# Clears cut into row slices, the lead's tap weights in the scans' PSUM banks, and one FFN group of the last image as a 1x1 convolution with VectorE taps

## The chip, the cores and the metric

The kernel runs on one core of one Trainium2 chip. The metric is device time in microseconds (us). Three runs of the kernel before gave 30005.71, 30010.10 and 30014.66 us, so the median is 30010.1 us. The profile comes from one more execution, which took 29956.3 us.

## The reference, cut to what matters

Eight images of 64 channels and 128x128 pixels pass through two layers. All arithmetic is float32.

```python
# layer 0: every pixel gets nine softmax weights; "high" is the negated weighted sum of its 3x3 window plus the pixel
h = leaky(conv3x3(x, w1, b1))
w_hp = delta_center - softmax(conv1x1(h, w2, b2), axis=1)
x = x + sum(shifted(x, k) * w_hp[:, k:k+1] for k in range(9))
# layer 1
x_norm = layernorm_over_channels(x)
seq = layernorm(tokens(x_norm))                      # 16384 tokens of 64 channels
for i in range(2):                                   # two blocks, each a scan forwards and one backwards
    seq = bimamba_block(seq, ...)                    # 128 inner channels x 16 states
x4 = conv3x3(image(rmsnorm(seq)), resconv_w) + res
dw = depthwise3x3(conv1x1(x_norm, dw1_w), dw2_w)
x = x + dw * x4
xn = layernorm_over_channels(x)
g = depthwise3x3(conv1x1(xn, ffn_in_w), ffn_dw_w)    # 64 -> 340 channels, each with its own nine taps
g1, g2 = split(g)                                    # 170 channels each
return x + conv1x1(gelu(g1) * g2, ffn_out_w)         # 170 -> 64
```

## The kernel before, in words

**Steps.** All work after the weights' preparation is entered into a table with `at(time, phase, fn)` and then issued in sorted order of time and phase. The phases are FEED, SCAN, MID, PROD, DECAY and REST, in that order. Each engine executes its own instructions in exactly this order, and so does the queue of SyncE (SP), which issues every DMA. A step has no fixed length: where an instruction waits, everything behind it on its engine waits too.

**Scans.** One image is 64 chunks of 16 steps (1024 steps). A chunk is 1024 tokens in one direction of one block. GpSimd (POOL) forms eight products per chunk (`drive`, L991), ScalarE (ACT) sixteen exponentials (`decay`, L999) into PSUM tiles of the pool `ps_w` (tag `w`, two tiles of 128x1024, each two banks), VectorE (DVE) sixteen scans (L1017 and L1019), and DVE or POOL multiplies with C (L1041, L1038). `dtx` (L947) overwrites a chunk's `dt` on POOL after that tile's copy to DRAM has landed.

**Front, Mix and FFN** are the convolutional stages. Each is 16 chunks of eight rows: two halves of 4x128 pixels, one on the lower 64 partitions and one on the upper 64. Front (layer 0 and the first norms) of image b+1, and Mix and FFN of image b, run beside scans. The exceptions are Front of image 0, which starts at step -199 while the first scan products start at step -5, and FFN of the last image, which starts at step 1084 of that image while its scans end at step 1024. Such a stage is called alone here.

**PSUM.** Beside the two `w` tiles there are four single banks: `y` (scan outputs), `mm` (projections), `bg` and `acc` (convolutional stages). A pool hands out a bank again once the last reader of the tile before is done.

**Front's taps.** For each of nine taps `weight` (L498 to L500) spreads one row of softmax weights over the channels with a matmul into the bank `bg`; `weighted` (L504) multiplies the shifted window with it on DVE; `gather` (L510) adds the product into `acc` with an identity matmul. `bg` also holds the tile `ms` of the norms.

**FFN.** The weights of 1x1 and depthwise convolution are multiplied into one 3x3 convolution from 64 to 340 channels. These come in groups: group 0 is the first 128 channels of g1, group 1 the first 128 of g2, and group 2 the remaining 42 of each. A window tile holds a window on its lower 64 partitions and the same window shifted by one pixel on the upper 64, so that one matmul makes two taps (`wpair`, L746) and the third is made from 64 partitions (`wlast`, L752). A float32 matmul stands as two records in the profile. Alone, a group's two PSUM halves lie in one `w` tile; order and times for a chunk that starts at step a are: group 0 at a, group 2 at a+3, GELU at a+5, group 1 at a+6, products with GELU's result at a+9, `project` (L777 to L786) at a+12. Chunks follow each other every 12 steps. The weights of a stage are one tile, `bgw`, loaded from DRAM by `load_weights` (L428).

**Clears.** Zero-padded images lie in DRAM as 64 channels of 131 rows of 130 pixels. `clear` (L88) writes zeros over a whole one with one DMA from a 130-wide tile: `x` first of all, `dw0` at step -199, `xm` at 64, `xn` at 128, `dw1` at 192.

## Time and profile before

| what | value |
|---|---|
| median of three runs | 30010.1 us |
| the profiled execution | 29956.3 us |
| its span in the profile | 29954.4 us |
| PE, DVE, ACT, POOL busy | 81%, 90%, 62%, 92% of the span |
| first scan product (L991) | 567.8 us after the span's start |
| FFN alone: first matmul to the span's end | 29447.9 to 29954.4 us |

Busy time is the time in which an engine had an instruction in work. A wait line names the engine and instruction that waited, what released it, the microseconds in total, how often, and the longest. A row of a stretch gives each engine's busy microseconds with its number of instructions, then the clock that TensorE was granted as a share of full speed, the mean busy share of the 16 DMA engines, and GB/s. Rows marked SPq are DMA issues. In a group's line "128*64 128x512" means a contraction over 128 partitions, 64 output partitions, and a moving operand of 512 columns.

### The profile page before, as it was taken

The numbers are of one execution on the slowest core, as the hardware profiler recorded it, in microseconds if no ns is written. First come the engines' busy times: TensorE is split into PE (matmuls) and PEld (weight loads), VectorE is DVE, ScalarE is ACT, GpSimd is POOL, SyncE is SP. The second block draws the span as 40 slices with busy tenths as digits, with TensorE's granted clock in tenths as the row PEclk, the third lists the DMA queues.
The fourth block names the chain that finished last, engine by engine and source line by source line (L and its number), as shares of the span: only waits on it lengthen the run. The fifth ranks groups of instructions, "written<-read, shape, count | busy, mean of one in ns | idle before, by whom it ended". The sixth has DMA issues, their size and how long they took to land. (4 is left out here: it accounts for less than half of the span.)

```text
span 29954.4 us, 307972 instructions
## 1 busy us (share of the span) xinstructions
PE 24257.7 (81%) x96344; PEld 8093.1 (27%) x96344; DVE 27086.6 (90%) x17258; ACT 18533.8 (62%) x28316; POOL 27661.8 (92%) x8732
## 2 busy tenths in 40 slices
PE   7666888878888788887888788887888878888579
PEld 3211232223322233222322223222232223322123
DVE  3899999999999999999999999999999999999992
ACT  2566666666666666666666666666666666666661
POOL 3999999999999999999999999999999999999991
PEclk8777888988989888988899889898898988889789
DMA  4776676766777677776777767776677766777672
GB/s 100 210 241 214 221 235 230 237 213 223 237 231 237 213 225 237 232 232 210 233 232 238 225 214 232 232 237 223 215 236 232 240 214 222 235 234 234 214 240 75
DMA packets 2529698, 6617.29 MB, mean 221 GB/s; under 512 B 417862, under 2 KB 722262, under 8 KB 2525750
## 3 DMA queue, kind: packets, MB, share of 16 engines
q1 hardware_dynamic: 2528054, 6597.59, 68.4%
q8 instruction: 761, 12.47, 0.2%
q14 instruction: 883, 7.23, 0.1%
HBM read 5363.40 MB, written 1266.10 MB: 221 GB/s over the span
## 5 line engine op out<-in xcount | busy, mean ns | idle before, releaser
L991 POOL TENSOR_TENSOR bu<-dup,bp 128x2048 f32<-128x2048 f32 x4096 | 18578.8, 4539 | 557.7 <-DVE w L1019 421.4
L999 ACT ACTIVATE w<-dtp,a_neg 128x1024 f32<-128x1024 f32 x8192 | 9162.3, 1118 | 510.2 <-DVE hs L1017 313.9
L1038 POOL TENSOR_TENSOR hs<-hs,cp 128x1024 f32<-128x1024 f32 x2832 | 6685.3, 2361 | 197.9 <-ACT state L1031 133.3
L1041 DVE TENSOR_TENSOR hs<-w,cp 128x1024 f32<-128x1024 f32 x5360 | 6564.9, 1225 | 310.9 <-DMA cp<-bc_dram 77.6
L1017 DVE TENSOR_TENSOR_SCAN w<-w,state,bu 128x1024 f32<-128x1024 f32 x2677 | 6280.9, 2346 | 346.5 <-ACT w L999 345.9
L1019 DVE TENSOR_TENSOR_SCAN w<-w,state,bu 128x1024 f32<-128x1024 f32 x2683 | 6291.0, 2345 | 314.1 <-ACT w L999 313.5
L1057 PE MATMUL y<-hs,sel_y 128*32 128x512 f32 x32768 | 5183.3, 702 | 33.0 <-POOL hs L1038 32.6
L1031 ACT COPY state<-w 128x1 f32<-128x1 f32 x5360 | 837.4, 156 | 5040.0 <-DVE hs L1041 5004.5
L1017 DVE TENSOR_TENSOR_SCAN hs<-w,state,bu 128x1024 f32<-128x1024 f32 x1419 | 3321.3, 2341 | 86.4 <-ACT w L999 36.9
L1019 DVE TENSOR_TENSOR_SCAN hs<-w,state,bu 128x1024 f32<-128x1024 f32 x1413 | 3307.7, 2341 | 52.8 <-ACT w L999 34.7
L1050 PE MATMUL y<-xc,dskip 128*64 128x512 f32 x4096 | 1622.3, 860 | 2025.6 <-ACT yv L1074 1339.3
L869 PE MATMUL xp<-hn,wx 128*128 128x512 f32 x4096 | 2269.2, 682 | 485.3 <-ACT xc L875 339.8
L746 PE MATMUL fp<-fw,bgw 128*128 128x512 f32 (+1 forms) x6144 | 2353.9, 638 | 64.7 <-ACT ga L759 63.5
L1057 PEld LDWEIGHTS y<-hs,sel_y 128*32 128x32 f32 x32768 | 736.8, 116 | 3496.6 <-issue 2469.7
L1031 ACT COPY state<-hs 128x1 f32<-128x1 f32 x2832 | 540.2, 191 | 1829.2 <-DVE hs L1019 929.6
L414 POOL TENSOR_TENSOR r<-r,neg_half 128x8 f32<-128x8 f32 x768 | 1263.5, 1645 | 380.5 <-ACT r L411 323.9
L875 ACT ACTIVATE xc<-xp,cbias 128x512 f32<-128x512 f32 x1024 | 697.2, 681 | 1415.1 <-PE xp L869 1414.7
L910 PE MATMUL dp<-xc,wdt 128*128 128x512 f32 x2048 | 1228.5, 684 | 351.8 <-ACT dt L917 268.2
L752 PE MATMUL fp<-fw,bgw 64*128 64x512 f32 (+1 forms) x6144 | 1501.1, 608 | 0.0
L999 ACT ACT_TABLE_LOAD x1134 | 1454.9, 1283 | 20.1
L947 POOL TENSOR_TENSOR dt<-dt,xc 128x1024 f32<-128x1024 f32 x512 | 1212.8, 2369 | 246.5 <-DMA dt_dram<-dt 223.8
L510 PE MATMUL acc<-t,ident 128*128 128x512 f32 x2304 | 1361.3, 675 | 0.0
(184 smaller groups left out, 26903.7 us busy)
## 6 DMA issues: line engine op xcount, KB each, us to landing
bp<-bc_dram SPq DMA_DIRECT2D x4096, 256.0 KB, 4.0
dup<-du_dram SPq DMA_DIRECT2D x4096, 256.0 KB, 5.0
dtp<-dt_dram SPq DMA_DIRECT2D x4096, 256.0 KB, 5.0
cp<-bc_dram SPq DMA_DIRECT2D x4096, 256.0 KB, 5.0
hn<-hn_dram SPq DMA_DIRECT2D x1024, 256.5 KB, 4.8
dt_dram<-dt SPq DMA_DIRECT2D x512, 512.0 KB, 3.1
du_dram<-dt SPq DMA_DIRECT2D x512, 512.0 KB, 2.6
yf_dram<-yv SPq DMA_DIRECT2D x512, 256.0 KB, 4.4
```

Of the source, the lines that this page charges most:

```text
L746: nc.tensor.matmul(o, wpair[:, i, g, m], self.win[h][:, i : i + ROWS, 0:W], start=(i == 0), stop=False)
L752: nc.tensor.matmul(o, wlast[rows, i, g, m], self.win[h][rows, i : i + ROWS, lo : W + lo], start=False, stop=(i == 2),)
L869: nc.tensor.matmul(self.xp[h], wx[:, self.l, self.d, i, :], self.hn2[:, s.start + 2 * i : s.stop + 2 * i], start=(i == 0), stop=(i == 1),)
L991: nc.gpsimd.tensor_tensor(bu, self.dup[self.pairs[k][1]], self.over_pair("bp", k), ALU.mult)
L999: nc.scalar.activation(w, self.dtp[gp][:, i, :], AF.Exp, scale=a_neg[:, self.l, self.d, g, j : j + 1])
L1017: nc.vector.tensor_tensor_scan(to, w, bu, s0, ALU.mult, ALU.add)
L1019: nc.vector.tensor_tensor_scan(to[:, ::-1], w[:, ::-1], bu[:, ::-1], s0, ALU.mult, ALU.add)
L1031: nc.scalar.copy(self.column(u), h[:, T - 1 : T] if self.d == 0 else h[:, 0:1])
L1038: nc.gpsimd.tensor_tensor(hs, hs, c, ALU.mult)
L1041: nc.vector.tensor_tensor(hs, w, c, ALU.mult)
L1050: nc.tensor.matmul(self.y[C * h : C * h + C, :], dskip[:, self.l, self.d, C * gp : C * gp + C], self.xc[:, s], start=True, stop=False,)
L1057: nc.tensor.matmul(self.y[lo : lo + 32, :], sel_y, hs[:, i, s], start=False, stop=(k % 4 == 3))
```

## The change

- **Clears.** `clear` takes a range of rows. Each of the four images is written in 15 DMAs of nine rows (the last has five): `dw0` from step -219 every 2 steps, `xm` from 64, `xn` from 192 and `dw1` from 320, every 8 steps.
- **Front.** The chunks 0 to 7 of image 0, whose taps end ahead of step -2, put two taps' weights into one tile of tag `w`, by halves, in place of `bg`.
- **FFN of the last image.** Group 2 is no longer a 3x3 convolution on TensorE. `before_taps` makes its 1x1 convolution over the six rows of both windows into four banks (`acc`, `bg`, `mm`, `y`), ACT copies them to SBUF, and DVE makes nine taps for each of the two sets of 42 channels. The residual is added by DVE in place of an identity matmul. Chunks follow every 8 steps, the weights are loaded at step 1074 in place of 1080, and their tile and its preparation hold the 1x1 weights and taps in addition.

```diff
-LAST_MIX_STEP, LAST_MIX_AT, LAST_FFN_STEP, LAST_FFN_AT = 16, 826, 12, 1084
+LAST_MIX_STEP, LAST_MIX_AT, LAST_FFN_STEP, LAST_FFN_AT = 16, 826, 8, 1084
...
-    def clear(img):
+    def clear(img, lo=0, hi=PW + 1):
         nc.sync.dma_start(
-            img.rearrange("c (r w) -> c r w", w=PW),
-            zero.rearrange("c (o w) -> c o w", o=1).to_broadcast([C, PW + 1, PW]),
+            img.rearrange("c (r w) -> c r w", w=PW)[:, lo:hi],
+            zero.rearrange("c (o w) -> c o w", o=1).to_broadcast([C, hi - lo, PW]),
         )
...
-    FRONT_W, MIX_W, FFN_W = 9 * 64 + P, 18 * P, 18 * P + 2 * C
+    FRONT_W, MIX_W, FFN_W = 9 * 64 + P, 18 * P, 18 * P + 2 * C + P + 2 * 9
...
+            if g == 2:
+                nc.scalar.copy(win_b[:, c0 : c0 + n], turned(fn[0:n, :], ident[0:n, 0:n], C, n)[0:C, 0:n])
+                for h in range(2):
+                    k0 = 9 * (c0 > 0)
+                    nc.sync.dma_start(wtap_b[C * h : C * h + n, k0 : k0 + 9], fd[r0 : r0 + n, :])
...
         def weight(self, k):
-            self.wb = bg_tile("wb")
+            if not self.alone:
+                self.wb = bg_tile("wb")
+            else:
+                if k % 2 == 0:
+                    self.wbs = pw.tile([P, T], F32, tag="w", name="wb")
+                self.wb = self.wbs[:, N * (k % 2) : N * (k % 2) + N]
+            self.wbk[k] = self.wb
...
+            self.alone = a + FRONT_STEP < -2
...
+        def before_taps(self):
+            _, _, _, _, win_b, _ = ffn_weights(Bg.weights)
+            self.banks = [acc_tile("f1"), bg_tile("f1"), mm_tile("f1"), py.tile([P, N], F32, tag="y", name="f1")]
+            for i, bank in enumerate(self.banks):
+                lo = C * (i < 2)
+                for h in range(2):
+                    r0 = 3 * (i % 2)
+                    nc.tensor.matmul(
+                        bank[C * h : C * h + C, 0 : 3 * PW], win_b[:, lo : lo + C],
+                        self.win[h][0:C, r0 : r0 + 3, :], start=True, stop=True,
+                    )
+
+        def before_taps_out(self):
+            self.pre = wk.tile([P, 2, T], F32, tag="hs", name="f1", bufs=3)
+            for i, bank in enumerate(self.banks):
+                lo = 3 * PW * (i % 2)
+                nc.scalar.copy(self.pre[:, i // 2, lo : lo + 3 * PW], bank[:, 0 : 3 * PW])
+
+        def taps(self, i):
+            _, _, _, _, _, wtap_b = ffn_weights(Bg.weights)
+            win = self.pre[:, i, 0 : (ROWS + 2) * PW].rearrange("p (r w) -> p r w", w=PW)
+            o = tmp("gt" if i == 0 else "ct")
+            for k in range(9):
+                w = wtap_b[:, 9 * (1 - i) + k : 9 * (1 - i) + k + 1]
+                if k == 0:
+                    nc.vector.tensor_scalar(as_rows(o), tap(win, k), w, None, ALU.mult)
+                else:
+                    nc.vector.scalar_tensor_tensor(as_rows(o), tap(win, k), w, as_rows(o), ALU.mult, ALU.add)
...
-                nc.tensor.matmul(o[h], wout_b[rows, :], self.gt[rows, :], start=False, stop=False)
-            nc.tensor.matmul(self.op, ident, self.o, start=False, stop=True)
+                nc.tensor.matmul(o[h], wout_b[rows, :], self.gt[rows, :], start=False, stop=self.alone)
+            if not self.alone:
+                nc.tensor.matmul(self.op, ident, self.o, start=False, stop=True)
 
         def add(self):
-            nc.scalar.copy(self.o, self.op)
+            if self.alone:
+                nc.vector.tensor_tensor(self.o, self.o, self.op, ALU.add)
+            else:
+                nc.scalar.copy(self.o, self.op)
...
             if self.alone:
-                groups = ((0, 0, self.first_out, 2), (3, 2, None, 0), (6, 1, self.times, 9))
-                gelus, out = 5, 12
+                at(a - 6, REST, self.before_taps)
+                at(a - 5, DECAY, self.before_taps_out)
+                at(a - 5, REST, self.taps, 0)
+                at(a - 2, REST, self.taps, 1)
+                groups = ((0, 0, self.first_out, 2), (3, 1, self.times, 6))
+                gelus, out = 3, 9
...
-        at(a - 4, REST, load_weights, 2)
+        at(a - (10 if step == LAST_FFN_STEP else 4), REST, load_weights, 2)
...
-    for t, img in ((FIRST_FRONT_AT, dw_img[0]), (64, xm_img), (128, xn_img), (192, dw_img[1])):
-        at(t, REST, clear, img)
+    rows = -(-(PW + 1) // NCH)
+    for t, step, img in ((FIRST_FRONT_AT - 20, 2, dw_img[0]), (64, 8, xm_img), (192, 8, xn_img), (320, 8, dw_img[1])):
+        for i in range(NCH):
+            lo, hi = rows * i, min(rows * i + rows, PW + 1)
+            if lo < hi:
+                at(t + step * i, REST, clear, img, lo, hi)
```

More of the change, by code (lines that the diff above doesn't have):

```diff
@@ L177, in ffn_weights @@
         v = t[:, 0 : 18 * P].rearrange("p (i r g m) -> p i r g m", i=2, r=3, m=P)
-        return v[:, 0], v[:, 1], t[:, 18 * P : 18 * P + C], t[:, 18 * P + C : FFN_W]
+        o = 18 * P + 2 * C
+        return v[:, 0], v[:, 1], t[:, o - 2 * C : o - C], t[:, o - C : o], t[0:C, o : o + P], t[:, o + P : FFN_W]
     with tc.tile_pool(name="wspill", bufs=1) as fp, tc.tile_pool(name="wprep", bufs=2) as pp, \
@@ L184 @@
         dw2, wres = mix_weights(wt[1])
-        wpair, wlast, wout_a, wout_b = ffn_weights(wt[2])
+        wpair, wlast, wout_a, wout_b, win_b, wtap_b = ffn_weights(wt[2])
         def twice(src, n, m, k=1):
@@ L436, in __init__ @@
             self.n1, self.n2, self.n3 = Norm(), Norm(), Norm()
-            self.t = {}
+            self.t, self.wbk, self.alone = {}, {}, False
         def load_x(self, name):
@@ L503, in weighted @@
             self.t[k] = tmp("t")
-            nc.vector.tensor_tensor(as_rows(self.t[k]), tap(self.xb, k), as_rows(self.wb), ALU.mult)
+            nc.vector.tensor_tensor(as_rows(self.t[k]), tap(self.xb, k), as_rows(self.wbk.pop(k)), ALU.mult)
         def gather(self, k):
@@ L726, in conv @@
         def conv(self, g, part):
-            wpair, wlast, _, _ = ffn_weights(Bg.weights)
+            wpair, wlast, _, _, _, _ = ffn_weights(Bg.weights)
             if part == 0 and self.alone:
@@ L755, in conv @@
                     )
+        def before_taps(self):
[24 more added lines that the diff above has]
+                    nc.vector.scalar_tensor_tensor(as_rows(o), tap(win, k), w, as_rows(o), ALU.mult, ALU.add)
+            if i == 0:
+                self.gt = o
+            else:
+                self.rest = [None, o]
         def first_out(self, h):
@@ L761, in gelus @@
         def gelus(self):
-            self.gt = tmp("gt")
-            nc.scalar.activation(self.gt, self.rest[0], AF.Gelu)
+            if self.alone:
+                nc.scalar.activation(self.gt, self.gt, AF.Gelu)
+            else:
+                self.gt = tmp("gt")
+                nc.scalar.activation(self.gt, self.rest[0], AF.Gelu)
             for h in range(2):
@@ L777, in project @@
         def project(self):
-            _, _, wout_a, wout_b = ffn_weights(Bg.weights)
+            _, _, wout_a, wout_b, _, _ = ffn_weights(Bg.weights)
             self.op = bg_tile("fo")
@@ L784, in project @@
                 rows = slice(C * h, C * h + REST_HID)
-                nc.tensor.matmul(o[h], wout_b[rows, :], self.gt[rows, :], start=False, stop=False)
-            nc.tensor.matmul(self.op, ident, self.o, start=False, stop=True)
+                nc.tensor.matmul(o[h], wout_b[rows, :], self.gt[rows, :], start=False, stop=self.alone)
+            if not self.alone:
+                nc.tensor.matmul(self.op, ident, self.o, start=False, stop=True)
         def add(self):
-            nc.scalar.copy(self.o, self.op)
+            if self.alone:
+                nc.vector.tensor_tensor(self.o, self.o, self.op, ALU.add)
+            else:
+                nc.scalar.copy(self.o, self.op)
         def store(self):
```

## The prediction

> **What bounds the kernel now.** The page's busy shares came first, then a table by stretch, then waits, chain and timeline of the stretches in which the change works. POOL's share only says that the scans, most of the span, run at POOL's pace:

> ```profile
> PE 24257.7 (81%) x96344; PEld 8093.1 (27%) x96344; DVE 27086.6 (90%) x17258; ACT 18533.8 (62%) x28316; POOL 27661.8 (92%) x8732
> ...
> 450.00:500.00 50.00, 40.72 (x149) 18.29 (x148) 10.30 (x18) 8.80 (x19) 5.82 (x6) 0.83 0.13 37
> ...
> 820.00:840.00 20.00, 11.30 (x53) 3.59 (x51) 19.80 (x12) 12.51 (x19) 9.78 (x6) 0.87 1.25 153
> 840.00:860.00 20.00, 7.75 (x18) 2.43 (x18) 3.76 (x3) 3.20 (x6) 11.14 (x5) 0.62 0.76 183
> ...
> 29500.00:29550.00 50.00, 48.31 (x158) 17.56 (x160) 3.95 (x6) 5.50 (x10) 0.00 (x0) 1.00 0.18 48
> ```

> The columns are PE, PEld, DVE, ACT, POOL, clock, DMA share, GB/s. Read three different limits: in the lead (450) PE is busy 41 of 50 us and DVE 10; at 820 to 860 POOL, normally full, loses some 20 us while the DMA engines are full; in the tail (29500) PE is alone at full clock, DVE at 8%. So DVE is free exactly where group 2's taps go.

> The chain shows one tail chunk, TensorE alone:

> ```profile
> 29458.11 5.30 PE fp L746 x24
> 29463.41 5.30 PE fp L752 x24
> 29468.72 5.35 PE fp L746 x12
> ...
> 29489.34 5.30 PE fp L746 x24
> ```

> A chunk repeats every 29489.34 - 29458.11 = 31.23 us. Group 2 (x24 and x24) takes 29468.72 - 29458.11 = 10.61. Waits and timeline of the clears (first image, first clear) and of the lead:

> ```profile
> POOL dt L947 <- DMA dt_dram<-dt: 19.1, 1, 19.1
> ...
> 812.88 0.60 SPq L89 DMA_DIRECT2D xm_dram<-zero  x1
> 816.28 22.15 SPq L517 DMA_DIRECT2D x_dram<-x  x1
> ...
> PE wb L500 <- DVE t L504: 13.4, 9, 7.2
> ...
> PE ms L405 <- DVE t L504: 5.2, 6, 0.9
> ```

> One clear holds the queue: the next issue needs 22.15 us, `dt`'s store behind it lands late, and POOL waits 19.1 us.

> **The change, part by part.**

> *FFN alone, TensorE.* In the timeline twelve 128*128 records take 5.24 us (29699.92 to 29705.16) and twelve 64*128 records, which overlap in pairs, 2.78 with the change of shape; a group is 8.02, two are 16.05. Before, `project` with its 0.86 us wait for DVE fills the rest, 31.23 - 10.61 - 16.05 = 4.6. After, group 0 of the next chunk stands between group 1 and `project`, so the products on DVE (2 x 0.69) are done under 8 us of matmuls. `project` without the identity is 8 records that overlap in pairs, 8 x 0.215 = 1.7, plus two changes of shape of 0.15: 2.0. `before_taps` is 8 matmuls, 16 records of 390 columns. The nearest row is

> ```profile
> L752 PE MATMUL fp<-fw,bgw 64*64 64x512 f32 x384 | 85.9, 592 | 0.0
> ```

> that is 24 records in 5.3 us, 0.22 each in pairs, so 16 x 0.22 x 390/512 = 2.7. The row's pairs use different input partitions, these the same ones; 128*64 records (group 2's first x24) share inputs and also take 5.30, so I take the paired price and keep 5.4 (unpaired) as bound. New wait: the second bank is `bg`, which `add` must read first, and `add` stands behind nine taps on DVE; behind the waiting matmul stand group 1 and all later chunks. Period: 16.05 + 2.0 + 2.7 = 20.8 plus this wait.

> *FFN alone, DVE.* A tap is 128x512 from SBUF. Nearest rows are

> ```profile
> 29437.49 0.75 DVE L664 SCALAR_TENSOR_TENSOR dwv<-cv,v_resconv_b,dwv 128x512 f32<-128x512 f32 x1 [18.49 <-PE cv L657]
> ...
> L771 DVE TENSOR_TENSOR ga<-ga,fp 128x512 f32<-128x512 f32 x32 | 20.6, 684 | 110.0 <-PE fp L752 110.0
> ```

> the same operation at 0.75 with a PSUM source; below, L1041's 1225 ns for 1024 columns minus L771's 684 for 512 gives 0.54 per 512 without fixed cost. I take 0.75 (same operation), plus 0.04 since each tap depends on the one before (the maximum at 174.77, 0.23 long, and its dependent subtraction at 175.04): 0.79. Walk from the end of group 1 of chunk c-1 (t=0): products to 1.5; nine taps of chunk c to 8.6; PE has group 0 of chunk c to 8.1 and `project` to 10.1; `add` 10.3 to 11.0; `before_taps`' first bank runs meanwhile, so PE waits about 0.3 and ends at 13.1; group 1 to 21.1. ACT copies two banks by 12.5, so the other nine taps end at 19.6, and the product with GELU's result (0.69) at 20.3. DVE is done 0.8 us ahead: hidden, and if a tap is dearer, the period grows only past 0.9 us. ACT's 9 operations (some 5 us by 0.59 each) have no share. Period 21.1.

> *Tail.* Weights are issued when the last Mix matmul ends (29436.4, not 29440.0 behind x2's store), but `before_taps` of chunk 0 comes ahead of group 0, which I put at 29450 in place of 29447.9. Group 0 cold 10.2 (as 29447.85 to 29458.04), `before_taps` 2.8, group 1 8.0: 29471. Then 14 x 21.1 and a last period without `before_taps` of 18.3: 29784.7. After group 1's end before (29937.32 + 8.2) the span had 8.9 left; without the identity 8.0: 29793. Gain 29954 - 29793 = 161. Bounds of the period: 20.4 (gain 172) and 23.8 (unpaired, gain 118).

> *Clears beside scans.* The three POOL waits are 19.1, 19.0 and 20.4, ordinary ones (the page's L947 group idles 246.5 us over 512) 0.5 each: 57 us go. Each clear took 31.3 to 35.1 us to land, so a nine-row slice is some 2.2 us of queue, 45 of them. A slice is issued at a chunk's steps 0 and 8, after the loads of those steps; the next POOL-critical store is issued at step 3 and needed at step 5. Bounds: nothing, or all 45 x 2.2 = 99 us exposed. Loads land in 4 to 5 us and are used two or more steps (6.5 us) on, so I take 0.1 each: 5. Net gain 52 (range -42 to 57). Next late is nothing: POOL stands at 50.00 of 50 us after the clears.

> [...]

> *Lead.* `dw0`'s 4.3 MB move ahead of the second `xa` load and stay ahead of the first `xb` load, which ends the wait at 192.98 either way; `xa` of chunk 1 lands some 15 us later, at about 180, and its hidden matmuls then end near 190, still under that wait: 0 (-5 to +4). The waits above give 5.2/6 = 0.9 and some 0.3 (the 0.8 us wait of the fifth tap, most of which passes to its gather, since odd taps still wait for their pair's reader) per chunk: 1.2 x 7 = 8. Preparation: two matmuls, two copies and four DMAs more, some 2 us. Net +6 (-8 to +14).

> **Sum.** 161 + 52 + 6 = 219. Against the profiled execution 29956.3 - 219 = 29737; it lies 53.8 us (0.18%) under the median, so the timed median becomes 30010.1 - 219 = 29791.

> **The rivals.**

> 1. *The new FFN stages are dearer* (taps at 1.2 us, or `before_taps` unpaired): DVE 18 x 1.2 + 1.4 + 1.4 + some 1.5 idle = 26 us a chunk, or PE 23.8. The tail then gains 85 or 118 in place of 161: 29834 to 29867. For it: no row has a tap with three SBUF operands. Against: 0.75 above.
> 2. *Slices expose their queue time:* net -42 to +20 in the middle, 29823 to 29885. For it: POOL's `dt` wait reacts to any queue. Against: only one in two slices is near that store.
> 3. *The spread is not freed:* two taps share a tile, so readers may still block as before: lead -2, 29799.
> 4. *Slower: TensorE's clock falls in the tail.* The lead's clock is 0.83 with 9 of 50 us idle, and a 128*128 matmul of 512 columns takes 2.07 us at 297.60 and 1.12 at 307.04. If the waits for banks halve the clock, 21.1 becomes 41: 16 x (41 - 31.2) = 157 lost, time 30010 + 157 - 58 = 30109. It decides from a period of 38.6 (31.2 + (58 + 60)/16), a clock near 0.55. Against: the tail held 0.98 to 1.00 with a 0.86 us gap per chunk; the new gaps are shorter.

> [...]

> **How the numbers follow.** Forecast 0.62 (own range 29765 to 29815), rival 1 0.16, rival 2 0.12, rival 3 0.06, rival 4 0.03, no change for a reason unseen 0.01. Low end: 172 + 57 + 14 = 243, 29767, and 15 us for the runs' spread and a colder start: 29750. High end takes in rivals 1 and most of 2: 29870. A measurement of this kernel tells 0.2% (60 us) from no change: faster 0.95, same 0.02, slower 0.03.

> **What would show it.** Right: in the tail a period near 21 us, PE still near 48 of 50 at clock 1.00, DVE near 38 of 50, taps at 0.75; no POOL wait over 5 us in `dtx` in the first image; first scan product some 6 us ahead of 567.8. Wrong: DVE full in the tail, PE waiting for DVE at the second bank, a clock under 0.9 there, or chunks of the first image longer by 2 us a slice.

## The result and the profile after

Four runs of the changed kernel took 29720.49 to 29750.91 us, median 29735.58; four of the kernel before 29997.28 to 30014.66, median 30007.90. The ratio is 0.9912 (95% interval 0.9900 to 0.9925): 272 us faster, where 219 had been forecast. The time lies 14 us under the low end of the range.

The profiled execution took 29750.91 us. Its page, and the same stretches by engine as before (PE, PEld, DVE, ACT, POOL, clock, DMA share, GB/s):

```profile
PE 24131.5 (81%) x95804; PEld 8066.2 (27%) x95804; DVE 27302.9 (92%) x17562; ACT 18550.1 (62%) x28366; POOL 27655.0 (93%) x8732
```

```profile
820.00:840.00 20.00, 16.13 (x78) 5.72 (x74) 19.77 (x15) 13.69 (x22) 20.00 (x8) 1.00 0.40 123
840.00:860.00 20.00, 12.25 (x40) 4.01 (x40) 16.67 (x9) 14.38 (x25) 20.00 (x8) 0.71 0.84 236
29550.00:29600.00 50.00, 49.72 (x168) 19.05 (x168) 36.75 (x53) 9.15 (x18) 0.00 (x0) 1.00 0.28 69
```

POOL no longer loses time at 820 to 860: 20.00 of 20 in both rows, after 9.78 and 11.14. In the tail DVE went from 2.66 of 50 us to 36.75, and PE is still the full engine at clock 1.00. The same stretch before:

```profile
29550.00:29600.00 50.00, 49.15 (x182) 17.24 (x180) 2.66 (x4) 6.00 (x11) 0.00 (x0) 1.00 0.12 32
```

The chain of one tail chunk, and the taps as a group (busy us, mean ns, idle before):

```profile
29560.81 1.01 PE fo L833 x4
29561.82 0.49 PE fo L836
29562.31 0.33 PE f L779
29562.64 0.21 PE fo L836 x2
29562.85 0.02 issue
29562.88 0.70 DVE o L842
29563.57 0.04 issue
29563.62 2.19 PE f L779 x12
29565.80 5.35 PE fp L760 x12
29571.15 2.78 PE fp L766 x12
29573.92 5.35 PE fp L760 x12
29579.27 2.78 PE fp L766 x12
29582.05 1.01 PE fo L833 x4
```

```profile
L799 DVE SCALAR_TENSOR_TENSOR ct<-f,bgw,ct 128x512 f32<-128x512 f32 x112 | 84.2, 752 | 4.0
```

The period is 29582.05 - 29560.81 = 21.24 us (31.23 before). Only one piece of it is not TensorE's: `add` (L842), for whose reading of `bg` the products of `before_taps` (L779) wait 0.76 us.

The waits of POOL from 780 to 2700 us hold the clears of the first image. Before, that view has a line `POOL dt L947 <- DMA dt_dram<-dt: 58.5, 3, 20.4`; after:

```profile
POOL bu L1050 <- DVE w L1078: 13.9, 19, 2.2
POOL dt L1006 <- DMA dt_dram<-dt: 6.4, 1, 6.4
```

and in the timeline of SP's queue the issue behind a slice takes 0.33 us, not 22.15:

```profile
816.24 0.60 SPq L89 DMA_DIRECT2D xm_dram<-zero  x1
818.14 0.33 SPq L530 DMA_DIRECT2D x_dram<-x  x1
```

To place the difference I cut every trace at first scan products (L991 before, L1050 after): the lead up to the first one of all, image 0, images 1 to 7, and the tail from the last chunk's first product to the end.

| us | lead | image 0 | images 1-7 | tail | span |
|---|---|---|---|---|---|
| before | 567.8 | 3615.1 | 25089.8 | 681.8 | 29954.4 |
| after | 571.1 | 3563.3 | 25091.9 | 522.9 | 29749.1 |
| difference | -3.3 | 51.8 | -2.1 | 158.9 | 205.3 |
| forecast | 6 | 52 | 0 | 161 | 219 |

The forecast of 0 for images 1 to 7 stands for the term that the sum doesn't have. So the two profiled executions differ by 205, and the medians by 272. The experiments had to say which of the two is the change, and where the other 67 lie.

### The profile page after: what moved, and what is told of

It is laid out like the page before. It is cut to its first block, busy times and chain, and to the rows that moved or that the text cites. A ratio compares the mean times of both kernels' runs of the same rounds, so it can differ in the third digit from the quotient of the medians.

```text
span 29749.1 us, 307276 instructions
## 1 busy us (share of the span) xinstructions
PE 24131.5 (81%) x95804; PEld 8066.2 (27%) x95804; DVE 27302.9 (92%) x17562; ACT 18550.1 (62%) x28366; POOL 27655.0 (93%) x8732
## 5 line engine op out<-in xcount | busy, mean ns | idle before, releaser
L1050 POOL TENSOR_TENSOR bu<-dup,bp 128x2048 f32<-128x2048 f32 x4096 | 18567.4, 4536 | 568.0 <-DVE w L1078 413.9
L1100 DVE TENSOR_TENSOR hs<-w,cp 128x1024 f32<-128x1024 f32 x5360 | 6564.4, 1225 | 322.3 <-DMA cp<-bc_dram 90.2
L760 PE MATMUL fp<-fw,bgw 128*128 128x512 f32 (+1 forms) x5760 | 2276.1, 642 | 66.1 <-ACT ga L807 64.7
L766 PE MATMUL fp<-fw,bgw 64*128 64x512 f32 (+1 forms) x5760 | 1415.6, 610 | 0.0
```

The costliest lines, as they stand in the source:

```text
L760: nc.tensor.matmul(o, wpair[:, i, g, m], self.win[h][:, i : i + ROWS, 0:W], start=(i == 0), stop=False)
L766: nc.tensor.matmul(o, wlast[rows, i, g, m], self.win[h][rows, i : i + ROWS, lo : W + lo], start=False, stop=(i == 2),)
L1050: nc.gpsimd.tensor_tensor(bu, self.dup[self.pairs[k][1]], self.over_pair("bp", k), ALU.mult)
L1100: nc.vector.tensor_tensor(hs, w, c, ALU.mult)
```

## The experiments

Each group was timed on one chip beside the kernel before. The chips are called A, B and C; the kernel before takes 30004 to 30006 us on A, 29998 on B and 29911 to 29919 on C. The chip of the first comparison isn't recorded; its timed runs are like those of A and B.

### One part at a time (chip A)

The kernel before unchanged, then with one part of the change each.

> The kernel before, unchanged, as a measure of what one kernel's executions differ by. The profiled execution of before took 29956.3 us and its timed ones 29997 to 30015, so a subtraction made against the one misses the other by about 54 us. Theory A (an execution's own condition: the profile of before happened to be short): this profile lies near 30005, and the extra time is in one stage of its trace. Theory B (profiling itself shortens an execution of before by about 50 us): this profile is again near 29956 with timed runs near 30006. Rival C (another chip): profile and timed runs agree within 15 us, at either level.

```diff
-    for t, img in ((FIRST_FRONT_AT, dw_img[0]), (64, xm_img), (128, xn_img), (192, dw_img[1])):
-        at(t, REST, clear, img)
+    for t, step, img in ((FIRST_FRONT_AT - 20, 2, dw_img[0]), (64, 8, xm_img), (192, 8, xn_img), (320, 8, dw_img[1])):
+        for i in range(NCH):
...
+                at(t + step * i, REST, clear, img, lo, hi)
```

> The kernel before with the sliced clears alone. The traces of before and after give the scans of image 0 as 51.8 us shorter, the lead not. If the clears hold only the queue for the time seen in the trace: 52 us gained (range 40 to 60), no dtx wait over 5 us. If the 54 us that the timed runs gained beyond the traces belong to the clears: about 105 us. If the slices' move in the lead costs time: some 5 us less than 52.

```diff
-            self.wb = bg_tile("wb")
+            if not self.alone:
+                self.wb = bg_tile("wb")
+            else:
+                if k % 2 == 0:
+                    self.wbs = pw.tile([P, T], F32, tag="w", name="wb")
+                self.wb = self.wbs[:, N * (k % 2) : N * (k % 2) + N]
```

> The kernel before with the tap weights in the scans' banks alone. My prediction's term: 8 us gained, by some 1.2 us of waiting per chunk. Rival (the clock gives it back: the trace of after shows half clock for 20.5 us of a 47.8 us chunk, before 17.1): within 3 us of no change, the waits for ms gone, chunk periods again 47.8 us. If the 54 us belong here: over 50 us.

```diff
-                groups = ((0, 0, self.first_out, 2), (3, 2, None, 0), (6, 1, self.times, 9))
-                gelus, out = 5, 12
+                at(a - 6, REST, self.before_taps)
+                at(a - 5, DECAY, self.before_taps_out)
+                at(a - 5, REST, self.taps, 0)
+                at(a - 2, REST, self.taps, 1)
+                groups = ((0, 0, self.first_out, 2), (3, 1, self.times, 6))
+                gelus, out = 3, 9
```

> The kernel before with the FFN change alone (taps, period 8, earlier weights). By the traces the tail is 158.8 us shorter and the preparation 5 us longer: 154 gained in all. If the 54 us that timed runs gained beyond the traces belong to the tail: about 208. The chunk period in the trace: 21.2 us in both cases; copies of x start at about 118 in place of 112.7 us.

| kernel | median | gain (ratio, interval) | lead | image 0 | images 1-7 | tail |
|---|---|---|---|---|---|---|
| before again | 30009.7 | -4 (0.9998, 0.9990 to 1.0007) | 597.0 | 3622.1 | 25106.9 | 681.7 |
| clears only | 29939.0 | 67 (0.9979, 0.9970 to 0.9988) | 569.7 | 3565.7 | 25115.5 | 682.2 |
| front only | 29973.0 | 33 (0.9990, 0.9981 to 0.9999) | 565.5 | 3618.7 | 25120.5 | 681.8 |
| FFN only | 29826.8 | 179 (0.9939, 0.9925 to 0.9952) | 586.9 | 3614.7 | 25098.8 | 524.6 |

The parts add up: 67 + 33 + 179 = 279. Each is above what was expected of it (52, 8 and 154), though each interval holds that (36 to 90, 3 to 57 and 144 to 225 us). The tail is worth 157 (681.7 against 524.6) and belongs to the FFN part; the first image is worth 56 (3622.1 against 3565.7) and belongs to the clears. What is new is the first row: the same kernel as in the profile before, with a lead of 597.0, not 567.8. Theory B is out, for this profile lies on its timed median. Theory A and rival C (another chip) both fit, though the extra time isn't in one stage: 29 us in the lead, 7 in image 0, 17 in images 1 to 7. Each wait of TensorE in its lead is as long as before (the longest 3.0, 1.5 and 0.8 us); the clock isn't the same. The stretch 200 to 500 us, first of the profiled execution before, then of this one:

```profile
200.00:500.00 300.00, 247.01 (x862) 110.14 (x860) 54.58 (x97) 52.82 (x114) 34.95 (x36) 0.80 0.13 37
```

```profile
200.00:500.00 300.00, 254.33 (x812) 111.75 (x810) 51.13 (x93) 46.46 (x102) 31.62 (x34) 0.74 0.12 33
```

812 matmul records in place of 862, at more busy time: clock 0.74 against 0.80.

### Does the clock set the lead? (chip C)

Short bf16 products, whose results nobody uses, fill TensorE's pauses in the chunks of the front alone, in the kernel before. Next to it, in the changed kernel, one thing undone or moved each: the spread back in `bg`; `dw0`'s slices behind the second `xa` load; the bank that waits for `add` taken last.

```diff
+        def warm(self, n):
+            w = py.tile([P, N], F32, tag="y", name="warm")
+            for _ in range(n):
+                nc.tensor.matmul(
+                    w, identb, identb.rearrange("p (o m) -> p o m", o=1).to_broadcast([P, N // P, P]),
+                    start=True, stop=True,
+                )
...
+            if a + 36 < 0:
+                for t, n in ((25, 3), (30, 8), (31, 3), (33, 2), (36, 5)):
+                    at(a + t, REST, self.warm, n)
```

> The kernel before, with 21 short bf16 matmuls per chunk of the lead put into TensorE's pauses (into the bank y, which nobody reads before step 0). Theory (the time the traces miss is TensorE's granted clock in the lead: same waits, but half clock for 140 us of 200 to 560 in the profile of before and 191 us in a second profile of the same kernel): the clock stays full, a chunk of the lead takes 40 to 44 us in place of 48 to 58, the first scan product comes at 515 to 540 us, and the median falls by 50 to 90. Rival 1 (the lead's pace is set by the waits for ACT and POOL): the extra matmuls cost some 4.5 us each chunk, the median rises by 20 to 35. Rival 2 (the difference between executions lies in the scans): no change beyond 20 us.

```diff
-            if not self.alone:
-                self.wb = bg_tile("wb")
-            else:
-                if k % 2 == 0:
-                    self.wbs = pw.tile([P, T], F32, tag="w", name="wb")
-                self.wb = self.wbs[:, N * (k % 2) : N * (k % 2) + N]
+            self.wb = bg_tile("wb")
```

> The changed kernel with the tap weights back in the bank bg. Theory (the front's change gains by a better clock in most executions, some 30 us as front_only measured): 15 to 40 us slower than the changed kernel's median 29736, a first scan product 15 to 30 us after 571. Rival (its gain is only the 1.2 us of waiting per chunk that the trace shows): 0 to 10 us slower.

```diff
-    for t, step, img in ((FIRST_FRONT_AT - 20, 2, dw_img[0]), (64, 8, xm_img), (192, 8, xn_img), (320, 8, dw_img[1])):
+    for t, step, img in ((FIRST_FRONT_AT + 9, 8, dw_img[0]), (64, 8, xm_img), (192, 8, xn_img), (320, 8, dw_img[1])):
```

> The changed kernel with the slices of dw0 from step -190 every 8 steps. The changed kernel's first tap waits for a window that stands behind 14 slices (196.0 us in the trace). If the slices are what delays it: first tap at 184 to 188, first scan product some 8 to 12 us earlier at an equal clock, median 5 to 15 lower. Rival (the copies of x hold the queue anyway): within 3 us.

```diff
-            self.banks = [acc_tile("f1"), bg_tile("f1"), mm_tile("f1"), py.tile([P, N], F32, tag="y", name="f1")]
+            self.banks = [acc_tile("f1"), mm_tile("f1"), py.tile([P, N], F32, tag="y", name="f1"), bg_tile("f1")]
```

> The changed kernel with the bank that add must read first (bg) taken last of the four by before_taps. If the wait for add is what lifts the period over the sum of the matmuls (20.8 forecast plus 0.3; measured 21.24): period 20.4 to 20.7, 8 to 13 us gained in the tail. Rival (the matmuls of 390 columns are themselves dearer than 0.22 x 390/512): period unchanged within 0.1.

| kernel | median | gain (ratio, interval) | lead | image 0 | tail |
|---|---|---|---|---|---|
| before, pauses filled | 29867.0 | 52 (0.9983, 0.9974 to 0.9991) | 528.1 | 3605.3 | 683.2 |
| after, spread in `bg` | 29693.6 | 225 (0.9924, 0.9911 to 0.9938) | 562.4 | 3554.0 | 524.3 |
| after, `dw0` later | 29682.0 | 237 (0.9921, 0.9907 to 0.9934) | 549.8 | 3558.1 | 524.7 |
| after, `bg` last | 29682.6 | 236 (0.9921, 0.9908 to 0.9935) | 551.5 | 3556.5 | 520.1 |

Filling the pauses adds work to TensorE and shortens the lead to 528. The stretch of 200 to 500 us, at clock 0.94:

```profile
200.00:500.00 300.00, 271.07 (x1111) 121.99 (x1112) 56.80 (x103) 63.05 (x134) 39.07 (x41) 0.94 0.15 42
```

The place of `dw0`'s slices is worth 2 us of lead (549.8 against 551.5), inside the -5 to +4 of the prediction and as the run's rival had it (within 3, not 8 to 12); the first tap comes at 182.7 us, and at 184.5 with the slices in their first place. The spread is worth 11 of lead in the traces (562.4 against 551.5). The medians don't show it: 29693.6 with the spread in `bg`, and 29693.8 for the changed kernel, timed later on this chip. With `bg` last the wait for `add` is gone from the chain, and the period is 29521.48 - 29500.60 = 20.88 us:

```profile
29500.60 1.01 PE fo L833 x4
29501.60 0.49 PE fo L836
29502.09 0.33 PE f L779
29502.42 0.19 PE fo L836 x2
29502.61 2.62 PE f L779 x14
29505.23 5.35 PE fp L760 x12
...
29521.48 1.01 PE fo L833 x4
```

That is 0.36 us less, not the 0.54 to 0.84 that was expected, for two records of `before_taps` had run inside the wait: 2.62 us for 14 of them in place of 2.19 for 12. The wait thus cost 16 x 0.36 = 5.8, and the tail shows 524.6 - 520.1 = 4.5, not 8 to 13.

### Both kernels on the same chip, and the sum of what helped (chip B)

The gains on chip C looked smaller than the 272 of the first comparison, so both kernels ran again unchanged, with the spread back in `bg` as before, and with a version that has late `dw0` slices, `bg` last and filled pauses.

> The kernel before once more, unchanged, on another occasion. Theory (the profiled execution of before and the timed median don't stand 53.8 us apart as a constant: the lead's granted clock differs from one execution to the next and moves the whole): ratio within 0.001 of 1; the images within 12 us of 3615.1, 3615.6, 3606.5, 3612.5 and the tail 681.7 +- 1, but the first scan product anywhere from 540 to 600 us, with less half-clock time between 200 and 560 us where it is early. Rival (the profiled execution of before was a chance fast one, and the rest are alike): first scan product within 3 us of the 597.0 of the first repeat.

> The changed kernel, unchanged, timed in the same rounds as the one before. Theory (the three parts are worth 160 in the tail, 52 to 60 in the first image, and the lead's share is that of the clock): gain 215 to 245 in the timed medians here, with a tail of 523 +- 2 and a first image some 52 us shorter than before's. Rival (the 272 between the first medians is the change's worth on any occasion): gain 260 to 280.

> The changed kernel with the front's spread weights back in their one bank, beside the unchanged changed kernel. Theory A (the move of the spread is worth its 5 to 8 us of waits, and the 33 us of the front part by itself were the clock's pace that day): within 12 us of the changed kernel, first scan product within 15 us of its. Rival (the move takes the lead out of a locked pace of 47.8 us per chunk and is worth 25 to 40): 25 to 40 us slower than the changed kernel, all of it ahead of the first scan product.

> The changed kernel with three additions: the bank that waits for the previous add is taken last, the slices of the first clear come later (not ahead of the second load of x), and in the chunks of the front alone 21 short products per chunk (results unused) fill TensorE's pauses. Theory (the lead's length is set by TensorE's granted clock, which the pauses lower): first scan product 20 to 40 us earlier than the changed kernel's, lead clock above 0.9, tail 520, so 30 to 55 us faster than the changed kernel. Rival (with the spread in its own buffers the lead is bound by loads and VectorE, and the clock no longer matters): first scan product within 8 us of the changed kernel's, 0 to 12 us faster in all.

| kernel | median | gain (ratio, interval) | lead | image 0 | images 1-7 | tail |
|---|---|---|---|---|---|---|
| before again | 29989.2 | 9 (0.9999, 0.9990 to 1.0008) | 584.4 | 3614.5 | 25117.2 | 682.6 |
| after again | 29737.4 | 260 (0.9913, 0.9899 to 0.9926) | 563.9 | 3550.8 | 25081.3 | 525.9 |
| after, spread in `bg` | 29750.8 | 247 (0.9917, 0.9903 to 0.9930) | 573.5 | 3557.6 | 25090.3 | 523.1 |
| after, all three | 29693.2 | 305 (0.9896, 0.9881 to 0.9911) | 517.9 | 3560.9 | 25091.4 | 521.0 |

Before's lead is 584.4 here, neither 567.8 nor 597.0, with tail and image 0 as ever: its executions differ, and the first profile's was not the only odd one. The gain of 260 is the rival's (260 to 280), not the 215 to 245 that I expected: 272 was no accident of the first timing (that it holds on any occasion, the last runs on chip C refute). The spread is worth 13 by the medians, whose runs overlap (29723.68 to 29751.82 and 29728.13 to 29764.70), and 10 in the lead; the 12 of theory A is missed by one, and the 25 to 40 of the rival are out. The version with all three is 44 faster than the changed kernel, its lead is 46 shorter (20 to 40 had been expected), and at clock 0.97:

```profile
200.00:500.00 300.00, 277.02 (x1162) 125.16 (x1160) 60.97 (x111) 69.27 (x142) 40.71 (x42) 0.97 0.25 56
```

### The change with the clock's swings taken out of the lead (chip C)

The filled pauses in both kernels, the front alone once more, and the changed kernel on chip C.

> The kernel before with 21 short products per chunk of the front alone in TensorE's pauses, once more. Theory (the lead's length follows the granted clock): 45 to 65 us faster than before, first scan product near 530 and the same within 5 us as on the other occasion (528.1).

> The changed kernel with the same short products in its lead, beside warm_before_2. Theory (the 40 to 50 us that the sum of 219 lacks are the clock's, in the lead of before's executions): with the swings out of both, the two differ by 205 to 232, first scan products within 10 us of each other. Rival (the change itself takes 20 to 40 us out of the lead): they differ by 240 to 275.

> The move of the spread alone, once more. Theory A (5 to 8 us of waits, the rest the clock's pace): 0 to 20 us faster than before, first scan product between 560 and 590. Rival (it takes the lead out of a slower pace): 25 to 45 us faster, first scan product at 562 to 570 again.

> The changed kernel unchanged, on the same chip as the other three. Theory: 25 to 45 us slower than warm_after, the difference all ahead of the first scan product; first scan product between 550 and 575; gain over before 215 to 265 by the chip. Rival (pauses in the lead no longer matter once the spread is moved): within 12 us of warm_after.

| kernel | median | gain (ratio, interval) | lead | image 0 | images 1-7 | tail |
|---|---|---|---|---|---|---|
| before, pauses filled | 29870.3 | 40 (0.9986, 0.9977 to 0.9995) | 524.2 | 3604.2 | 25059.2 | 682.7 |
| after, pauses filled | 29661.4 | 249 (0.9917, 0.9903 to 0.9930) | 515.1 | 3556.7 | 25071.6 | 524.8 |
| front only | 29893.7 | 17 (0.9996, 0.9987 to 1.0004) | 555.6 | 3597.2 | 25048.2 | 682.8 |
| after again | 29693.8 | 217 (0.9926, 0.9913 to 0.9940) | 551.6 | 3553.1 | 25054.8 | 524.6 |

On this chip the change is worth 217, the sum of the prediction to 2 us, and with filled pauses in both kernels (clock 0.96 before and 0.95 after, from 200 to 500 us, where the changed kernel without them has 0.78) 29870.3 - 29661.4 = 209, as the theory had it (205 to 232). Filling the pauses is worth 32 in the changed kernel, 36.5 of it in the lead (551.6 to 515.1), so the pauses still count once the spread is moved. In the kernel before it brought 40, less than the 45 to 65 expected. The spread alone brings 17 by the medians, which theory A had (0 to 20), with an interval that holds zero; its lead of 555.6 is shorter than either theory had it, as every lead on this chip.

### Before once more, and the best version once more (chip A)

> The kernel before, unchanged, a third time. Theory (before's extra time on two of the chips lies in the lead and in the images after the first, and its tail and first image are fixed): tail 682 +- 1, first image 3596 to 3622; if the chip is one where before takes near 29915, first scan product 550 to 572, and images 1 to 7 together 25040 to 25075; if one near 30000, first scan product 568 to 600 and images 1 to 7 at 25085 to 25125.

> The changed kernel with last bank, late slices of the first clear and filled pauses in the lead, a second time. Theory (the filled pauses are worth 30 to 45, the bank 4, the slices little): first scan product near 517, tail 521, gain over before 250 to 310 by the chip, that is 30 to 50 more than the changed kernel's there.

Before took 30005.8 (ratio 1.0001, 0.9992 to 1.0010), with lead 573.8, image 0 3621.5, images 1 to 7 25104.8 and tail 681.2, all as expected for a chip where it takes near 30000. The version with all three took 29703.3, ratio 0.9899 (0.9885 to 0.9912): 301 faster than before, lead 521.5, tail 518.9. No other version reached a lower ratio than this one's 0.9896 and 0.9899.

## Why the prediction was wrong

**Tail: right.** 161 forecast, 158.9 in the first pair, 157 to 160 in the other pairs. Term by term, on the chain: project 1.01 + 0.49 + 0.21 = 1.71 us (2.0 forecast); `before_taps` 0.33 + 2.19 = 2.52 (2.7), and 0.33 + 2.62 = 2.95 where no wait hides a part (`bg` last), so the paired price was near and the unpaired 5.4 is out; the wait for `add` 0.76 (0.3), which `bg` last removes. These make 4.99 us, and the forecast's 2.0 + 2.7 + 0.3 make 5.0: the sum is that near because the errors cancel. Two groups take 16.26 (16.05), so the period is 21.24 (21.1). A tap takes 752 ns, and eight dependent ones 6.26 us together, 0.78 each (0.79). DVE at 36.75 of 50 (near 38) doesn't limit. Rivals 1 and 4 are out: the tap is not 1.2, and the clock stayed at 1.00.

**Clears beside scans: right in kind and nearly in size.** 52 forecast, 51.8 in the first pair; the waits of `dtx` went from 58.5 us to 6.4. The one that is left is over the 5 us of the prediction's sign (3.6 and 4.6 in the changed kernel's repeats, 4.9 with the clears alone). By chip: 56 on A (3622.1 against 3565.7), 64 on B (3614.5 against 3550.8), 44 and 47.5 on C (3597.2 against 3553.1, 3604.2 against 3556.7), where image 0 is shorter before the change too. Rival 2 is out: it had at most 20 us gained, and the rows show no more queue time than that one wait. Slices of 292.5 KB in place of one clear of 4257.5 KB freed the queue at the price of one wait of 3.6 to 6.4 us.

**Lead: right in kind, too small.** The waits moved as forecast. Before, TensorE's waits from 200 to 500 us have these two lines:

```profile
PE wb L500 <- DVE t L504: 5.4, 7, 0.8
PE ms L405 <- DVE t L504: 5.2, 6, 0.9
```

The changed kernel's have neither, and one new one, the last:

```profile
PE dwp L551 <- ACT ha L460: 18.1, 6, 3.0
PE rb L427 <- POOL r L421: 9.2, 6, 1.5
PE cp L534 <- ACT dwt L555: 4.7, 6, 0.8
PE ms L412 <- ACT sq L538: 4.1, 6, 0.7
PE ms L412 <- ACT hc L539: 3.6, 6, 0.6
PE acc L523 <- DVE t L517: 3.2, 6, 0.6
```

The net is 7.4 us for six chunks, 1.2 each, as forecast, so rival 3 is out. In the leads of the traces the spread showed 10 and 11 us where the program was otherwise equal (chips B and C), against 8; the medians show 13 on B, with overlap, and nothing on C. But in the first pair the changed kernel's lead was 3.3 us longer, not 6 shorter, at a lower clock (0.77 against 0.80) and with its first tap 3.0 us later (196.0 against 193.0).

**The failed step: "it lies 53.8 us (0.18%) under the median, so the timed median becomes 30010.1 - 219 = 29791".** It takes the 53.8 us for a constant between profile and timing that the changed kernel has too, and so the terms read from that one execution for the worth of the change on any. Neither held. The changed kernel's two profiled executions on the first chip and on B (29750.9 and 29723.7 us) lie 15 above and 14 below their medians. Three more of the kernel before (30009.7, 30000.6 and 29983.1) lie at, 11 above and 23 below theirs. The first one's 29956.3 lies below the whole range of timed runs of that kernel on A and B (29976.7 to 30028.2) and above the range on C (29884.9 to 29938.6). Whether it was a short execution or one on another chip stays open, since its chip isn't recorded.

What the sum lacked can be read by terms. The mean of the three others less that of the changed kernel's two is 157 in the tail (161 forecast), 62 in image 0 (52), 18 in the lead (6) and 23 in images 1 to 7, for which the sum had no term: 260 us, as timed on B. So the terms for the lead and image 0 were too small by 12 and 10, that for the tail too large by 4, and a term of 23 was missing. That 29956.3 - 219 = 29737 comes within 2 us of the measured time is luck: the gain against the timed kernel before is 272, not 219. On chip C the timed gain is 217, the forecast sum.

Where that execution is short can be read too. Against the mean of the three others it is 17 us shorter in the lead (567.8 against 585.1), 4 in image 0 and 20 in images 1 to 7 (25089.8 against 25109.6). In the lead this is mostly the granted clock: for the four executions of the same instructions the lead follows the clock of 200 to 500 us in order, 0.80, 0.79, 0.77, 0.74 and 567.8, 573.8, 584.4, 597.0. Some 5 us lie ahead of the first tap (193.0 us, 196.8 to 199.0 in the others). The middle two are

```profile
200.00:500.00 300.00, 248.35 (x852) 110.29 (x851) 54.17 (x97) 52.55 (x113) 33.27 (x35) 0.79 0.13 37
```

```profile
200.00:500.00 300.00, 249.01 (x834) 111.47 (x834) 51.88 (x93) 51.08 (x111) 33.25 (x35) 0.77 0.12 34
```

From the first tap to the first scan product the changed kernel takes 375.1 us against 387.6 at a clock of 0.77, and 369.0 against 374.8 at 0.79 to 0.80 (two executions of before): 6 to 13 less, around the forecast 8. With the pauses filled on chip C, its whole lead is 9 shorter (515.1 against 524.2).

**What stays open.** The gain is 217 on C, 260 and 272 elsewhere; the three intervals overlap (common part 0.9913 to 0.9925, that is 225 to 261 us), so a single worth near 240 isn't excluded. With the first profile and every other cut trace of A and B, with and without the part concerned, the terms are 158 for the tail, 58 for image 0, 13 for the lead (580.8 in four executions of before, 567.5 in two of after) and 17 for images 1 to 7 (25109.1 in six executions with the old tail and 25092.2 in five with all of the change or most of it), 246 together. The last 17, or 23, have no cause that I can name: of the change, only the larger load of FFN weights lies in these images, the ranges overlap, and on C there is no such difference (25052 and 25054). Why the kernel before had a lower clock in its leads on A and B (0.74 to 0.79) than in the first profile (0.80) is open too.

## What to carry to other kernels

A sum of terms read from one execution is a difference: before it is set against a median, that execution has to be placed among others of the same kernel, stretch by stretch, and where it lies below them in a stretch, the term for that stretch is read from the others too. A large clear (4257.5 KB here) on a queue that also carries the pipeline's stores was worth cutting: the slices of 292.5 KB left one wait of 3.6 to 6.4 us, and one whole DMA stopped the queue for 22 us. Where TensorE has only short pauses (3.0 us at most here) and yet a low granted clock (0.74 to 0.80 from 200 to 500 us here), a few unused products in the pauses can be worth more (32 to 52 us here, at a clock of 0.94 to 0.96) than removing waits of other causes (10 us of lead).

## What the runs showed of the hardware that was not expected

**The lead has its own pace, and it goes with the granted clock.** In the first profile the first taps of chunks 3 to 6 of the front alone lie 47.8 us apart, and a chunk repeats as one stretch at full and one at half clock:

```profile
397.80:428.52 30.72, 25.70 (x107) 11.67 (x106) 6.99 (x13) 4.58 (x12) 4.18 (x5) 1.00 0.12 33
428.52:445.59 17.07, 13.50 (x39) 6.22 (x39) 1.97 (x3) 4.22 (x8) 1.64 (x1) 0.50 0.19 51
```

In the repeat with the lead of 597.0 they lie 50.6 to 58.4 us apart from chunk 1 on, and a stretch of 51.2 us there holds two such pairs:

```profile
382.88:396.54 13.66, 9.96 (x44) 4.44 (x44) 0.69 (x1) 3.84 (x9) 2.23 (x3) 1.00 0.19 48
396.54:413.60 17.06, 13.75 (x39) 6.02 (x39) 2.01 (x4) 3.94 (x7) 1.64 (x1) 0.50 0.19 54
413.60:427.26 13.66, 12.08 (x42) 5.62 (x42) 4.77 (x7) 0.27 (x1) 1.64 (x1) 1.00 0.00 1
427.26:434.08 6.82, 6.55 (x23) 3.08 (x22) 1.49 (x5) 0.98 (x3) 0.31 (x1) 0.50 0.16 51
```

**Chips differ by 0.3%.** The kernel before takes 29911 to 29919 us on one chip and 29998 to 30006 on two others, and some 57 of the 90 us lie in images 1 to 7 (25052 against 25109, the means with the old tail above). The tail, TensorE alone, is the same within 2 us on all (681.2 to 683.2).
